# A two-layer graph network on one core: how the first batch's nodes and masks are brought in

## The chip, the cores and the metric

The kernel runs on one core of a Trainium2 chip. The core has five engines with queues of their own: TensorE (PE in the profile, with its weight loads as PEld), VectorE (DVE), ScalarE (ACT), GpSimd (POOL) and SyncE (SP). SP and ACT also issue transfers between DRAM and the core's memory, which 16 DMA engines carry out. The metric is the device time of one execution in microseconds; lower is better.

## The reference, cut to what matters

The input is x, 8 batches of 2048 nodes with 256 features, and adj, one 2048 x 2048 matrix of zeros and ones (int32) shared by all batches. The first layer is attention with 4 heads of 64. Its keys are cut into 8 chunks of 256, and each chunk has a softmax of its own:

```
q, k, v = x @ WqT + bq, x @ WkT + bk, x @ WvT + bv
scores = clip(q . k / 8, -10, 10)
scores = where(mask == 0, -10, scores)         # mask: adj by chunks
attn = softmax(scores, over the 256 of a chunk)
ctx = sum over chunks of attn @ v
x1 = layernorm(x + layernorm(ctx @ WoT + bo + x) * gamma + beta)
```

The second layer is a graph attention: Wh = x1 @ W, an edge score from the two nodes' own factors (sums of Wh times a_src and a_dst), a softmax over the neighbours where adj is not zero, an elu, a residual and a last layernorm.

## The kernel before, in words

The 16 tiles of 128 nodes are handled in 4 groups of 512. For every batch there is a projection per group (`project`): x is brought in with the features on the partitions (xT), and three matrix products make kT, the values (vaug) and qT. Then a loop of 64 slots runs over (query group q, pair of heads hp, key chunk c). In a slot, `scores` multiplies kT and qT into PSUM (ps), VectorE clips and masks with a slab of int8 limits (pr, line 382), ScalarE takes the exponential, and `product` multiplies with vaug (pc, line 406), which ScalarE copies out as raw; `normalize` divides (rd on VectorE, then a multiplication and an addition on GpSimd). Beside the slots, `Between` does the output projection and the two layernorms of the query group that went before. From batch 1 on the slots also carry the second layer of the batch before, line 722 and its tiles e; in batch 0 they don't.

In batch 0 the slots carry the masks instead. Both layers need adj turned, in two forms in DRAM: clipD, int8 limits of plus or minus 80 for the first layer, by query group, and edgeD, zeros and ones for the second. The class `Masks` makes them in 48 pieces (t, m): a piece is tile row t of adj and one of three banks m of 6, 5 and 5 column tiles. One call of `step` sends the stores of the piece before (SP), loads a new piece (SP, araw), turns an older piece on TensorE (pm, line 236), evicts it twice (clip on VectorE, line 238; edge on ScalarE, line 240), and compares a third piece with zero into bf16 (ab, line 226, on VectorE). A piece is loaded two steps before it is compared, and compared one step before it is turned. The pieces go row by row: t outermost, m inside.

The order of instructions on every engine is written out by hand: each engine runs them as the program issues them, and no scheduler moves them. The part ahead of the slots, the prologue, is at the end of the function: it calls load, turn, and the three products of each group in turn, with a mask step after nearly every piece, 17 steps in all, and then `finish_constants`. That function folds a_src and a_dst into eight more columns of the second layer's weights (lines 167 and 168, VectorE), and the value bias into bo and beta (four matmuls, line 178, and lines 185 and 189 on VectorE). After it come the loads of the first three slabs, and `scores(0)`.

x is loaded in the prologue as in later batches by `load_turned` (line 269): eight transfers of 64 KB per group, in runs of 32 floats, which put every square of 32 x 32 in its turned place. One VectorE transpose of such squares (`turned`, line 281) then completes xT. The kernel has a second way, `transposed` (lines 284 to 294), which it uses once in each batch for x1: the nodes lie plainly on the partitions, TensorE turns eight squares of 128 x 128 into PSUM, and ScalarE copies them out (line 293). `load_x` (line 260) is the plain load, one transfer of 512 KB, used for the residual.

Of the kernel before, what the change touches and what calls it, by code (L numbers as in the profile page):

```python
# [13 lines left out]
AF = mybir.ActivationFunctionType  # L14
ALU = mybir.AluOpType
# [7 lines left out]
def adj_resnorm_kernel(  # L23
# [19 lines left out]
    nc = tc.nc  # L43
    B, N, F = x.shape
    H, D = a_src.shape
    NT = N // P
    NCH = N // CH
# [8 lines left out]
    QT = CH // P  # L56
    CLIP = 10.0 * 8.0
    FAR = 100.0
    BANKS = (6, 5, 5)
# [103 lines left out]
    def finish_constants():  # L163
        for k, a_sb in enumerate(aa):
            for c in range(KC):
                wa = small.tile([P, F], F32, tag="ee", name="wa")
                nc.vector.tensor_mul(wa, w1_sb[:, c, :F], a_sb)
                nc.vector.tensor_reduce(
                    w1_sb[:, c, F + k * H : F + (k + 1) * H],
                    wa.rearrange("p (h d) -> p h d", h=H),  # L170
                    AX.X,
                    ALU.add,
                )


        pb0 = psM.tile([P, CH], F32, tag="psM", name="pb0")
        for c in range(KC):
            nc.tensor.matmul(
                pb0[:, :F],
                lhsT=bv_sb[:, c : c + 1].to_broadcast([P, P]),  # L180
                rhs=wo_sb[:, c, :],
                start=(c == 0),
                stop=(c == KC - 1),
            )
        nc.vector.scalar_tensor_tensor(
            bo_sb, pb0[:, :F], float(NK), bo_sb, op0=ALU.mult, op1=ALU.add
        )

        nc.vector.tensor_sub(beta_sb, beta_sb, bo_sb)
# [4 lines left out]
    def send():  # L194
        while outgoing:
            outgoing.pop(0)()


    class Masks:
# [1 line left out]


        def __init__(self):
            self.pieces = [(t, m) for t in range(NT) for m in range(len(BANKS))]
            self.raw, self.bits, self.done = [], [], []
            self.next = 0

        def step(self):
            send()
            if self.next < len(self.pieces):  # L210
                t, m = self.pieces[self.next]
                n, j0 = BANKS[m], FIRST[m]
                araw = ep.tile([P, WIDE * P], I32, tag="e", name="araw")
                nc.sync.dma_start(
                    out=araw[:, : n * P], in_=adj[t * P : (t + 1) * P, j0 * P : (j0 + n) * P]
                )
                self.raw.append((t, m, araw))
                self.next += 1
            if self.bits:
                t, m, ab = self.bits.pop(0)  # L220
                self.turn(t, m, ab)
            if len(self.raw) > 2 or (self.raw and self.next == len(self.pieces)):
                t, m, araw = self.raw.pop(0)
                w = BANKS[m] * P
                ab = small.tile([P, WIDE * P], BF16, tag="hh", name="ab")
                nc.vector.tensor_scalar(ab[:, :w], araw[:, :w], 0, None, ALU.not_equal)
                self.bits.append((t, m, ab))

        def left(self):
# [2 lines left out]
        def turn(self, t, m, ab):  # L232
            n, j0 = BANKS[m], FIRST[m]
            pm = psL.tile([P, WIDE, P], BF16, tag="psL", name="pm")
            for k in range(n):
                nc.tensor.transpose(pm[:, k, :], ab[:, k * P : (k + 1) * P], identb)
            clip = small.tile([P, WIDE, P], I8, tag="ee", name="clip")
            nc.vector.tensor_scalar(clip[:, :n], pm[:, :n], 2 * CLIP, -CLIP, ALU.mult, ALU.add)
            edge = small.tile([P, WIDE, P], U8, tag="hp", name="edge")
            nc.scalar.copy(edge[:, :n], pm[:, :n])  # L240
            q, u = t // QT, t % QT
            mi = max(k for k in range(len(BANKS)) if FIRST[k] <= t)
            at = (t - FIRST[mi]) * P

            def stores():
                nc.sync.dma_start(
                    out=clipD[q][:, j0 : j0 + n, u * P : (u + 1) * P], in_=clip[:, :n]
                )
                nc.sync.dma_start(out=edgeD[mi][:, j0 : j0 + n, at : at + P], in_=edge[:, :n])

            outgoing.append(stores)


    def by_node(dram, b, g):

        return dram[b, g * CH : (g + 1) * CH, :].rearrange("(t p) f -> p t f", p=P)

    def load_x(b, g, name):
        t = blocks.tile([P, QT, F], F32, tag="xb", name=name)
        nc.sync.dma_start(out=t, in_=by_node(x, b, g))  # L260
        return t

    def load_squares(dst, src):


        for c in range(src.shape[1] // P):
            for a in range(P // SQ):
                f0 = c * P + a * SQ
                nc.sync.dma_start(
                    out=dst[a * SQ : (a + 1) * SQ, c, :].rearrange("r (k s) -> r k s", s=SQ),  # L270
                    in_=src[:, f0 : f0 + SQ].rearrange("(k r) s -> r k s", r=SQ),
                )

    def load_turned(dram, b, g, name):
        t = blocks.tile([P, KC, CH], F32, tag="xb", name=name)
        load_squares(t, dram[b, g * CH : (g + 1) * CH, :])
        return t

    def turned(t, name):
        dst = blocks.tile([P, KC, CH], F32, tag="xT", name=name)  # L280
        nc.vector.transpose(dst.rearrange("p c n -> p (c n)"), t.rearrange("p c n -> p (c n)"))  # L281
        return dst

    def transposed(src, name):

        dst = blocks.tile([P, KC, CH], F32, tag="xT", name=name)
        pt = two_banks([P, KC, CH], "pt")
        for c in range(KC):
            for k in range(QT):
                nc.tensor.transpose(  # L290
                    pt[:, c, k * P : (k + 1) * P], src[:, k, c * P : (c + 1) * P], identf
                )
        nc.scalar.copy(dst, pt)  # L293
        return dst

    def project(b, g):

        cols = slice(g * CH, (g + 1) * CH)
        st = {}

        def load():
            st["x"] = load_turned(x, b, g, "xp")

        def turn():
            st["xT"] = turned(st["x"], "xT")

        def linear(dst, w, bias, apart=False):
            if apart:
                pps = [psL.tile([P, CH], F32, tag="psL", name="pp") for _ in range(KC)]
            else:  # L310
                pp = two_banks([P, KC, CH], "pp")
                pps = [pp[:, c, :] for c in range(KC)]
            for c in range(KC):
                for kc in range(KC):
                    nc.tensor.matmul(  # L315
                        pps[c],
                        lhsT=w[:, kc, c * P : (c + 1) * P],
                        rhs=st["xT"][:, kc, :],
                        start=(kc == 0),
                        stop=(kc == KC - 1),  # L320
                    )
            for c in range(KC):
                nc.scalar.activation(
                    dst[:, c, cols], pps[c], AF.Identity, bias=bias[:, c : c + 1]
                )

        def values():
            pv = two_banks([P, QT, F], "pv")
            for u in range(QT):
                for kc in range(KC):  # L330
                    nc.tensor.matmul(  # L331
                        pv[:, u, :],
                        lhsT=st["xT"][:, kc, u * P : (u + 1) * P],
                        rhs=wv_sb[:, kc, :],
                        start=(kc == 0),
                        stop=(kc == KC - 1),
                    )
            nc.scalar.copy(
                vaug[:, QT * g : QT * (g + 1), :, :D],
                pv.rearrange("p t (h d) -> p t h d", h=H),  # L340
            )

        return [
            load,
            turn,
            lambda: linear(kT, wk_sb, bk_sb),
            values,
            lambda: linear(qT, wq_sb, bq_sb, b > 0 and g == NCH - 1),
        ]
# [459 lines left out]
    masks = Masks()  # L809
    groups = [project(0, g) for g in range(NCH)]  # L810
    groups[0][0]()
    for _ in range(2):
        masks.step()
    groups[1][0]()
    for g in range(NCH):
        for k, piece in enumerate(groups[g][1:]):
            if k == 1 and 0 < g < NCH - 1:
                groups[g + 1][0]()
            piece()
            if g or k:  # L820
                masks.step()
    finish_constants()

# [41 lines left out]
    for b in range(B):  # L867
# [15 lines left out]
        for s in range(SLOTS):  # L883
            q, hp, c = where[s]
# [157 lines left out]
```

## Time and profile before

| what | value |
| --- | --- |
| median of 3 runs | 3862.64 us (3862.37 to 3863.09) |
| the profiled execution | 3862.74 us, of which its span 3861.0 us |
| busy share of the span | PE 96%, DVE 83%, ACT 51%, POOL 36% |
| TensorE's granted clock, mean | 0.991 |
| first matmul | 17.74 us after the span's start |
| first slot's first pr | 80.23 us |
| scores of the third slot | 88.65 us |
| slots with a mask step, first query group | 4.5 to 4.6 us each |
| mask comparison (line 226) | 48 times, 0.48 us for 640 columns, 0.55 for 768 |
| clip (line 238) and edge (line 240) | 0.82 and 0.68 us for 640 columns |
| normalization on GpSimd (lines 428, 430) | 1.05 and 1.28 us in a slot |

The span is the time from the first to the last instruction, and the execution is a little longer than it. Times within the profile count from the span's start. In a timeline a line gives the start, the duration, the engine and line, the operation with what it writes and reads, the number of instructions merged, and in brackets the idle time before it with what ended that. ACTq and SPq are the sequencers that issue transfers; the duration there is that of the issue, not of the transfer. Matmuls are pipelined and their ends modelled, so the start of the next instruction says more than the duration.

### The profile page before, as it was taken

To read this page: it belongs to the slowest core of one execution; us is meant where nothing else is said; L and a number is where in the kernel's file an instruction comes from. 1 tells how busy PE (TensorE), PEld (TensorE's weight loads), DVE (VectorE), ACT (ScalarE), POOL (GpSimd) and SP (SyncE) were. 2 spreads that over 40 slices of the span, in tenths; PEclk is the share of its full clock that TensorE was granted. 3 is DMA by queue.
4 is the path that set the end of the run, shared out by engine and by line. 5 is a ranking of instruction groups with operands and counts; after the bars stand their busy time and mean duration, and the time that the engine had idled before them with its cause. 6 is when DMAs were issued, how large, how long until landed. Compare 5 with 4: busy or idle time off the path is not lost. (4 is left out here: it accounts for less than half of the span.)

```text
span 3861.0 us, 160222 instructions
## 1 busy us (share of the span) xinstructions
PE 3687.8 (96%) x72068; PEld 2746.0 (71%) x72068; DVE 3204.6 (83%) x4810; ACT 1953.6 (51%) x3601; POOL 1387.4 (36%) x1202
## 2 busy tenths in 40 slices
PE   7999999999999999999999999999999999999787
PEld 4656677776777777776777767777677777776676
DVE  3877499986999779995999959998699977998798
ACT  3666445554555555554555545555455555555321
POOL 0445233332433333433433324343243333344310
PEclk9999999999999999999999999999999999999999
DMA  7642333333433333333433334333343433333344
GB/s 148 154 109 62 83 101 96 97 89 98 112 101 100 80 121 102 102 94 73 140 96 100 99 87 135 96 98 87 103 111 99 103 80 118 102 102 86 92 147 123
DMA packets 771328, 398.48 MB, mean 103 GB/s; under 512 B 442576, under 2 KB 735824, under 8 KB 770640
## 3 DMA queue, kind: packets, MB, share of 16 engines
q1 hardware_dynamic: 720640, 354.54, 36.3%
q10 hardware_dynamic: 50000, 33.70, 2.7%
q8 instruction: 563, 9.22, 1.0%
q14 instruction: 125, 1.02, 0.1%
HBM read 331.22 MB, written 56.89 MB: 101 GB/s over the span
## 5 line engine op out<-in xcount | busy, mean ns | idle before, releaser
L382 DVE SCALAR_TENSOR_TENSOR pr<-ps,slab 128x1024 f32<-128x1024 f32 x1024 | 1192.1, 1205 | 208.8 <-PE ps L371 206.7
L702 DVE SCALAR_TENSOR_TENSOR e<-srow,gd,et 128x640 f32<-128x640 f32 (+1 forms) x1536 | 1349.6, 934 | 17.9 <-DMA et<-edgeD 12.5
L406 PEld LDWEIGHTS pc<-vaug,pr 128*64 128x64 f32 x32768 | 1040.6, 138 | 445.5 <-issue 245.3
L406 PE MATMUL pc<-vaug,pr 128*64 128x65 f32 x32768 | 1157.9, 224 | 42.6 <-ACT raw L413 35.1
L394 ACT ACTIVATE pr<-pr 128x1024 f32<-128x1024 f32 x1024 | 1053.0, 1058 | 184.5 <-DVE pr L382 168.4
L722 PE MATMUL pa<-waug,e 128*64 128x65 f32 x32768 | 1081.5, 224 | 42.4 <-DVE e L702 40.0
L722 PEld LDWEIGHTS pa<-waug,e 128*64 128x64 f32 x32768 | 1020.1, 139 | 68.1 <-DVE e L702 39.8
L371 PE MATMUL ps<-qT,kT 64*128 64x512 f32 x4096 | 1027.4, 619 | 6.8 <-DVE pr L382 6.5
L428 POOL TENSOR_TENSOR part<-raw,rd 128x512 f32<-128x512 f32 x448 | 469.5, 1048 | 1462.1 <-DVE rd L421 1449.7
L413 ACT COPY raw<-pc 128x260 f32<-128x260 f32 x1024 | 384.9, 376 | 1157.7 <-PE pc L406 1132.2
L430 POOL TENSOR_TENSOR acc<-acc,part 128x512 f32<-128x512 f32 x448 | 574.9, 1283 | 35.1
L371 PEld LDWEIGHTS ps<-qT,kT 64*128 64x128 f32 x4096 | 351.3, 186 | 330.4 <-issue 209.7
L421 DVE RECIPROCAL rd<-raw 128x8 f32<-128x8 f32 x512 | 101.1, 197 | 116.7 <-ACT raw L413 113.0
L428 POOL TENSOR_TENSOR acc<-raw,rd 128x512 f32<-128x512 f32 x64 | 66.9, 1045 | 352.8 <-DVE rd L421 352.0
L750 ACT ACTIVATE hh<-pa,dn 128x64 f32<-128x64 f32 x512 | 114.4, 320 | 100.7 <-DVE dn L746 96.9
L315 PE MATMUL pp<-xT,wk_sb 128*128 128x512 f32 x256 | 124.1, 630 | 36.9 <-DVE xT L281 36.9
L565 PE MATMUL pw<-w_sb,x1T 128*128 128x264 f32 x512 | 138.7, 406 | 17.0 <-ACT x1T L293 9.0
L481 POOL TENSOR_TENSOR rs_c<-rs_c,nhalf 128x4 f32<-128x4 f32 x32 | 55.6, 1738 | 226.9 <-DVE off_c L480 226.9
L521 PE MATMUL po<-wo_sb,qT 128*128 128x256 f32 x512 | 125.5, 389 | 2.1 <-DVE qT L448 1.5
L315 PEld LDWEIGHTS pp<-xT,wk_sb 128*128 128x128 f32 x256 | 49.8, 200 | 94.3 <-issue 73.1
L315 PE MATMUL pp<-xT,wq_sb 128*128 128x512 f32 x256 | 116.0, 596 | 0.0
L331 PE MATMUL pv<-wv_sb,xT 128*128 128x256 f32 x512 | 115.9, 379 | 0.0
(90 smaller groups left out, 1885.1 us busy)
## 6 DMA issues: line engine op xcount, KB each, us to landing
et<-edgeD SPq DMA_DIRECT2D x256, 320.0 KB, 3.2
slab<-clipD SPq DMA_DIRECT2D x512, 128.0 KB, 3.6
et<-edgeD SPq DMA_DIRECT2D x128, 384.0 KB, 3.5
srow<-rowD SPq DMA_DIRECT2D x64, 320.0 KB, 4.4
xp<-in_x_dram SPq DMA_DIRECT2D x256, 64.0 KB, 2.3
xg<-in_x_dram SPq DMA_DIRECT2D x32, 512.0 KB, 4.7
x1D<-y ACTq DMA_DIRECT2D x32, 512.0 KB, 3.1
x1g<-x1D SPq DMA_DIRECT2D x32, 512.0 KB, 5.7
```

What stands on the lines that cost most here:

```text
L315: nc.tensor.matmul(pps[c], lhsT=w[:, kc, c * P : (c + 1) * P], rhs=st["xT"][:, kc, :], start=(kc == 0), stop=(kc == KC - 1),)
L371: nc.tensor.matmul(ps[:, k, :], lhsT=kT[rows, hp, t * P : (t + 1) * P], rhs=qT[rows, hp, cols], start=True, stop=True,)
L382: nc.vector.scalar_tensor_tensor(pr, pss[u], -CLIP, slab[:, u, :].unsqueeze(1).to_broadcast([P, 2, CH]), op0=ALU.max, op1=ALU.min,)
L394: nc.scalar.activation(pr, pr, AF.Exp, scale=0.125)
L406: nc.tensor.matmul(pc[z * D : (z + 1) * D, i, :], lhsT=probs[s][u][:, k, i * P + z * D : i * P + (z + 1) * D], rhs=vaug[:, KT * c + u, 2 * ...
L413: nc.scalar.copy(raws[s][:, k], pc)
L428: nc.gpsimd.tensor_mul(part, raw[:, :, :, :D], rd.to_broadcast([P, 2, QT, D]))
L430: nc.gpsimd.tensor_add(accv, accv, part)
L521: nc.tensor.matmul(po[:, k, :], lhsT=qT[:, c, t * P : (t + 1) * P], rhs=wo_sb[:, c, :], start=(c == 0), stop=(c == KC - 1),)
L565: nc.tensor.matmul(pw[:, k, : F + 2 * H], lhsT=self.x1T[:, c, u * P : (u + 1) * P], rhs=w1_sb[:, c, :], start=(c == 0), stop=(c == KC - 1),)
L702: nc.vector.scalar_tensor_tensor(e[:, :w], self.rows[n][:, :w], self.gd[:, h, j : j + 1], self.edge[k // JG][:, j % JG, :w], op0=ALU.max, ...
L722: nc.tensor.matmul(self.pa[z * D : (z + 1) * D, i * D1 : (i + 1) * D1], lhsT=e[:, i * P + z * D : i * P + (z + 1) * D], rhs=self.waug[:, j ...
```

## The change

It touches batch 0 alone. First, x is loaded plainly and turned by TensorE with `transposed` in the four projections of batch 0; other batches keep `load_turned`. The first two groups' loads are issued ahead of the first mask pieces. Second, the comparison of masks moves from VectorE to GpSimd and is turned around (equal to zero instead of not equal), so the clip's constants change sign, and the edge eviction becomes an activation that computes 1 - value. Third, the pieces go bank by bank within a query group: four tile rows of bank 0, then of bank 1, then of bank 2, then the next group. Fourth, no mask step follows the turning of a group, which leaves 14 steps in the prologue, and `finish_constants` is called between groups 2 and 3.

```diff
         def __init__(self):
-            self.pieces = [(t, m) for t in range(NT) for m in range(len(BANKS))]
+            self.pieces = [
+                (t, m) for q in range(NCH) for m in range(len(BANKS)) for t in range(QT * q, QT * (q + 1))
+            ]
...
-                nc.vector.tensor_scalar(ab[:, :w], araw[:, :w], 0, None, ALU.not_equal)
+                nc.gpsimd.tensor_scalar(ab[:, :w], araw[:, :w], 0, None, ALU.is_equal)
...
-            nc.vector.tensor_scalar(clip[:, :n], pm[:, :n], 2 * CLIP, -CLIP, ALU.mult, ALU.add)
+            nc.vector.tensor_scalar(clip[:, :n], pm[:, :n], -2 * CLIP, CLIP, ALU.mult, ALU.add)
...
-            nc.scalar.copy(edge[:, :n], pm[:, :n])
+            nc.scalar.activation(edge[:, :n], pm[:, :n], AF.Copy, bias=1.0, scale=-1.0)
...
         def load():
-            st["x"] = load_turned(x, b, g, "xp")
+            st["x"] = load_turned(x, b, g, "xp") if b else load_x(b, g, "xp")
 
         def turn():
-            st["xT"] = turned(st["x"], "xT")
+            st["xT"] = turned(st["x"], "xT") if b else transposed(st["x"], "xT")
...
     groups[0][0]()
+    groups[1][0]()
     for _ in range(2):
         masks.step()
-    groups[1][0]()
     for g in range(NCH):
         for k, piece in enumerate(groups[g][1:]):
             if k == 1 and 0 < g < NCH - 1:
                 groups[g + 1][0]()
             piece()
-            if g or k:
+            if k:
                 masks.step()
-    finish_constants()
+        if g == 2:
+            finish_constants()
```

## The prediction

> **What bounds the kernel now.** I read, in this order, the page, busy time by stretch, the ordered timeline of the first 90 us, the waits of those 90 us, and two slots of the first batch's loop. By the page TensorE is busy 96% of the span in 40 slices of which only the first and the last three fall clearly short of full.
>
> ```profile
> PE 3687.8 (96%) x72068; PEld 2746.0 (71%) x72068; DVE 3204.6 (83%) x4810; ACT 1953.6 (51%) x3601; POOL 1387.4 (36%) x1202
> ...
> PE   7999999999999999999999999999999999999787
> ```
>
> So time lost or won on TensorE before batch 1 should move the end one for one; the change touches nothing later. Busy time by stretch (columns: stretch, its length, PE, PEld, DVE, ACT, POOL busy, granted clock, DMA share, GB/s):
>
> ```profile
> 0.00:20.00 20.00, 2.26 (x3) 1.17 (x4) 1.80 (x2) 1.28 (x1) 1.34 (x10) 1.00 0.83 175
> ...
> 60.00:80.00 20.00, 14.88 (x65) 8.51 (x65) 10.76 (x21) 7.51 (x11) 0.00 (x0) 1.00 0.78 172
> 80.00:100.00 20.00, 18.49 (x254) 11.46 (x256) 14.00 (x19) 11.63 (x17) 3.45 (x4) 0.83 0.35 74
> 100.00:150.00 50.00, 50.00 (x877) 33.62 (x871) 40.47 (x56) 36.87 (x55) 24.25 (x21) 1.00 0.69 156
> ```
>
> TensorE is idle for nearly 18 us at the start and about 5 us around 77 to 82 us, then full. The timeline says what ends those gaps:
>
> ```profile
> 8.38 1.07 ACTq L160 DMA_DIRECT2D a_sb<-in_a_dst_dram  x1
> 9.48 1.28 ACT L323 ACT_TABLE_LOAD   x1 [9.48 <-DMA gamma_sb<-in_gamma_dram]
> ...
> 16.44 1.25 DVE L281 STREAM_TRANSPOSE xT<-xp 128x1024 f32<-128x1024 f32 x1 [16.44 <-DMA xp<-in_x_dram]
> ...
> 17.74 6.00 PE L315 MATMUL pp<-xT,wk_sb 128*128 128x512 f32 x8 [17.74 <-DVE xT L281]
> ```
>
> The eight 64 KB pieces of x (4096 packets of 128 bytes) land last; ScalarE has been free since 10.8. And where the loop starts:
>
> ```profile
> 72.81 1.38 SPq L358 DMA_DIRECT2D slab<-clipD  x3
> ...
> 79.89 0.43 DVE L189 TENSOR_TENSOR beta_sb<-beta_sb,bo_sb 128x256 f32<-128x256 f32 x1
> 80.23 2.35 DVE L382 SCALAR_TENSOR_TENSOR pr<-ps,slab 128x1024 f32<-128x1024 f32 x2
> ...
> 81.51 3.79 PE L371 MATMUL ps<-qT,kT 64*128 64x512 f32 x8 [4.98 <-DVE pr L382]
> ```
>
> The first softmax tile waits behind finish_constants on VectorE (74.86 to 80.2), and the scores after it take 3.79 us where later ones take 1.99. The waits of these 90 us add the third loss, at each change of group:
>
> ```profile
> PE pm L236 <- DVE ab L226: 4.2, 3, 1.5
> ```
>
> **What the Trainium skill says.** "GPSIMD Engine Reference", Engine selection, calls one-input elementwise work there roughly line rate, and its Performance pitfalls give 1.0 to 2.0 cycles per element for compare bodies; at the page's 1.2 GHz that is, as an estimate, 0.5 to 1.3 us for 640 or 768 elements. The trace has no such operation. "ScalarE: Activation LUTs", What ACT_TABLE_LOAD costs: 1283 ns, plus about 1380 ns of drain; the trace agrees with the first (1.28), and shows nothing queued close behind the load, so not the second. "TensorE: Matmul & The Clock Gate", Why this matters for your kernels: keep idle gaps under about 3 us; here a 4.98 us gap was followed by halved speed, a 3.21 us gap at 317 us was not (the scores right after took 1.99).
>
> **The change, part by part**, on the profiled execution's own time, 3862.74 us (span 3861.0 and 1.74 around it; median of the runs shown 3862.64, so 0.1 lower).
>
> *Start.* One plain 512 KB load replaces eight small-packet loads: SP's 13.4 us of issuing become about 1, and VectorE's 1.25 us transpose becomes eight TensorE transposes (1.09 us) and one ScalarE copy (1.01 us, 1.06 from its start to the next matmul; both rows exist at 436 to 438 us). x no longer comes last, but the copy is ScalarE work, and ScalarE first issues its 13 loads and loads its table. In the changed program's order, DMA completions rotate through eight semaphores: bv's issue waits for the first x, gamma's for the second, w1's for the first mask piece, a_dst's for the second mask piece. By then four SP loads (1.84 MB) and four weights (1.05 MB) have moved, 2.9 MB. The trace moved 204 GB/s on average from 2.6 to 12 us, with slices up to 345. Counted from 2.6 us that ends at 11 to 17; I take 13.3, since large packets fill the engines better. Then a_dst 0.8, table 1.28, copy 1.06: first matmul at 16.4 instead of 17.74, **−1.3** (ends: 14.3, −3.4; 21.5 at the slow rate and with the drain, +3.8). The loads of groups 1 to 3 take SP 5.5, 4.4 and 5.0 us now and about 0.5 each after; behind them stand mask loads and stores, for which TensorE does not wait, so that is worth nothing. Uncovered it would be worth their difference, 13 us.
>
> *Three changes of group.* Before, from the last query matmul to the next key matmul: 2.91, 2.98 and 3.11 us, of which two mask pieces (0.45 each), the comparison and the transpose. After: one mask piece (0.45 to 0.5), then transposes to +1.6; ScalarE does its two query evictions (to about +1.35), the edge eviction (0.58 to 0.7) and the copy (1.06), which gives +3.05 to +3.15. At the third, finish_constants' four matmuls (1.08) come first: +3.9. Sum **+1.1** (ends 0 and +3). The comparison, 48 × 0.48 or 0.55 = 24 us of VectorE, is on GpSimd, idle here from 2 us on.
>
> *finish_constants.* Its 5.5 us of VectorE, one wait for a mask store included, go between two clips some 7 us apart, where VectorE has nothing else; without that gap they would hold the next clip, and cost at most 5.5. The first pr then waits for its slab: issued 0.44 us before the last query matmul ends (73.25), landed about 3.9 later, 3.6 after that end where it is now 7.0. **−3.4** (ends −5, −1.5). TensorE's gap shrinks to about 2.3 us, so its clock should hold: warm, the third scores follow the first pr by 6.3 us, now 8.4 (80.23 to 88.65): **−2.1** (ends −2.1, 0).
>
> *Mask pieces.* 14 instead of 17 steps in the prologue, so 37 instead of 34 in the loop. What a step costs there is seen from two slots:
>
> ```profile
> 97.65 1.99 PE L371 MATMUL ps<-qT,kT 64*128 64x512 f32 x8
> ...
> 102.11 1.99 PE L371 MATMUL ps<-qT,kT 64*128 64x512 f32 x8
> ```
>
> 4.46 us with a piece, against 3.94 between scores at 304.52 and 308.46 without: 3 × 0.52 = **+1.6** (the pieces' matmuls in the prologue are already taken out above). Bank by bank, a slab needs at most pieces stored one slot (4.5 us) before its own issue; stores land in 2.2 us, so this order costs nothing; if one were late, a slot would lose about 2 us once. The inverted clip and edge constants change no shape.
>
> *Loop with the comparison moved.* GpSimd works 1.05 + 1.28 of each 4.55 us slot. For the comparison I take 1.1 us (between the skill's ends; the two-input rows here, 2.0 to 2.5 ns per element, bound it at 1.3 to 1.9). 3.4 fits in 4.55. Behind it queue the next normalization, on whose reading of raw ScalarE waits two slots later. VectorE gains 0.5 us a slot, yet TensorE is full there: of its waits for the mask slots (3.5 us for edge, 1.0 for pr) I give **−0.4** (ends −3, +3).
>
> Sum: −1.3 + 1.1 − 3.4 − 2.1 + 1.6 − 0.4 = −4.5; 3862.74 − 4.5 = 3858.2, against the median 3858.1.
>
> **Rivals.** (1) *GpSimd becomes the bound.* If a comparison takes more than 4.55 − 2.33 = 2.2 us, each of some 36 slots stretches by the excess. At 2.35 us the gain is gone, at 2.55 the kernel is slower by over 0.2%, at 3.0 it takes 3858 + 36 × 0.8 = 3887. For it: GpSimd here needs 1.0 to 2.0 us for a power of four elements a partition, so some operations are slow there. Against: its masked select of 128 elements takes 0.29 us, 1.5 ns per element after a memset's 0.1 us floor. (2) *The start really is freed.* If loads overlap so well that x's transposes and ScalarE's table set the time, the first matmul comes at 9.48 + 1.28 + 1.06 + 0.1 = 11.9: 4.5 more, 3853.6. Against it stands the order of semaphores. (3) *The loop start stays cold or the slabs late* (first pr at +5.5, clock halved): 4 us of gain go, 3862.
>
> **How the numbers follow.** Likeliest 0.70: 3858.1, own range 3853.8 to 3862. Rival 1: 0.12, rival 2: 0.09, rival 3: 0.09. About 0.2%, 7.7 us, is what a measurement of this kernel can tell from no change: faster means under 3854.9, slower over 3870.4. Rival 2 and a tenth of the likeliest lie below: 0.16. Rival 1 above its 2.55 us and a little for the unforeseen: 0.12. The rest, 0.72, is the same. The range 3852.5 to 3865 leaves out rival 1's upper part and the tails.
>
> **What would show it.** Right: the first L315-type matmul at 15 to 18 us, released by ScalarE's copy, with the table load just before that; first pr at 3.4 to 4 us after the last query matmul, released by its slab's DMA; the next scores at 2 us, granted clock near 1.0 from 80 to 100; slots with masks still 4.5 us; GpSimd's comparison near 1.1 us. Wrong: a comparison over 2.2 us with ACT raw waiting for POOL, or the first matmul before 13 or after 20 us, or VectorE's pr slowed beside GpSimd.

## The result

The changed kernel takes 3857.56 us (median of four runs, 3856.91 to 3860.71), the kernel before, run beside it, 3862.86; the ratio is 0.9988, 95% interval 0.997 to 1.0005. Four runs leave the sign open. Run again, 18 times against 38, it takes 3856.91 us against 3862.29: **ratio 0.9986, interval 0.9979 to 0.9993**. The change makes the kernel faster by 0.14%, some 5.4 us. The forecast was 3858.1, a gain of 4.5.

The profiled execution is the slowest of the first four, 3860.71 us with a span of 3858.9; the profile of the second set has a span of 3854.7. Executions of one kernel differ by several microseconds (3854.69 to 3861.87 in the second set), so what follows counts differences at the same point of the prologue and not between ends.

The page of the changed kernel (busy time of each engine, share of the span, instructions):

```profile
PE 3696.8 (96%) x72100; PEld 2759.2 (72%) x72100; DVE 3178.8 (82%) x4758; ACT 1955.9 (51%) x3605; POOL 1475.8 (38%) x1250
```

TensorE has 32 more matmuls (the transposes), VectorE 52 fewer instructions (48 comparisons and four transposes), GpSimd 48 more. Busy time by stretch of the changed kernel (columns: stretch, its length, PE, PEld, DVE, ACT, POOL busy, granted clock, DMA share, GB/s):

```profile
0.00:20.00 20.00, 6.17 (x14) 3.46 (x15) 0.00 (x0) 2.29 (x2) 5.59 (x12) 1.00 0.74 230
20.00:40.00 20.00, 18.09 (x75) 11.32 (x74) 2.87 (x3) 8.14 (x11) 6.06 (x3) 0.91 0.38 84
...
80.00:100.00 20.00, 20.00 (x371) 13.95 (x369) 13.89 (x17) 14.14 (x22) 13.83 (x10) 1.00 0.56 120
```

The last row is what the forecast promised: 80 to 100 is full at a granted clock of 1.00, where it was 18.49 us busy at 0.83. The second is not: the clock is 0.91 from 20 to 40, where it was 1.00 in the kernel before:

```profile
20.00:40.00 20.00, 17.98 (x71) 10.65 (x70) 6.27 (x9) 7.69 (x11) 0.00 (x0) 1.00 0.71 129
```

The timeline of the changed kernel (start, duration, engine and line, operation, number merged, idle before it and what ended that; lines in between are left out here and below) shows the three places. The start:

```profile
5.85 1.94 PE L292 MATMUL pt<-identf,xp 128*128 128x128 f32 x8 [5.85 <-DMA xp<-in_x_dram]
12.27 1.12 ACTq L160 DMA_DIRECT2D a_sb<-in_a_dst_dram  x1
13.41 1.28 ACT L295 ACT_TABLE_LOAD   x1 [13.41 <-DMA gamma_sb<-in_gamma_dram]
14.71 1.01 ACT L295 COPY xT<-pt 128x1024 f32<-128x1024 f32 x1
15.77 5.36 PE L318 MATMUL pp<-xT,wk_sb 128*128 128x512 f32 x8 [7.99 <-ACT xT L295]
```

x has landed and is turned by 7.8 us; then TensorE waits 7.99 us for a copy that ScalarE can't begin, because its queue is still issuing constants. Those issues wait until earlier transfers have landed: bo's, at 9.57, for the value weights (landed at 9.55), and a_dst's, at 12.27, for the second mask piece (landed at 12.24). A change of group:

```profile
28.25 0.50 PE L238 MATMUL pm<-identb,ab 128*128 128x128 bf16 x6
...
30.48 1.01 ACT L295 COPY xT<-pt 128x1024 f32<-128x1024 f32 x1
31.54 5.40 PE L318 MATMUL pp<-xT,wk_sb 128*128 128x512 f32 x8 [1.91 <-ACT xT L295]
```

Between the two stand the transposes (28.58) and the copy. The same eight matmuls take 3.70 us in the last group; here they ran at reduced speed. And the start of the loop:

```profile
73.02 0.44 PE L238 MATMUL pm<-identb,ab 128*128 128x128 bf16 x5
...
76.05 4.81 DVE L385 SCALAR_TENSOR_TENSOR pr<-ps,slab 128x1024 f32<-128x1024 f32 x4 [1.73 <-DMA slab<-clipD]
77.33 2.26 PE L374 MATMUL ps<-qT,kT 64*128 64x512 f32 x8 [1.66 <-DVE pr L385]
```

The first pr is released by its slab and not by VectorE's other work, and the scores after it run at nearly full speed (2.26 us where it was 3.79). Put together, at the third scores (88.65 before, 82.07 now) the kernel is ahead by 6.58 us:

| part, from where to where | before, us | after, us | difference |
| --- | --- | --- | --- |
| span's start to first key matmul | 17.74 | 15.77 | -1.97 |
| first key matmul to last query matmul's end | 55.51 | 57.25 | +1.74 |
| that end to the first pr | 6.98 | 3.03 | -3.95 |
| first pr to the third scores | 8.42 | 6.02 | -2.40 |

The second row holds the changes of group (3.29, 3.05 and 3.33 us, before 2.91, 2.98 and 3.11: +0.67), the slow product (+1.70) and a first key product of 5.36 instead of 6.00 us (-0.64), which sum to +1.73.

The column of before is one execution, and it is a late one. In the two other kernels here that start as the kernel before does (the constants moved alone, the order of the pieces alone) the first key matmul comes at 16.68 and 17.03 us; in the six that start as the changed one it comes at 15.75 to 16.33. By these means the start is worth 1.1 us and not 1.97. The kernel with the order alone, which has the old start and the old loop's start, reaches its third scores at 87.45 us; against it the changed kernel is ahead by 5.4 us and not by 6.58.

In the loop the comparison on GpSimd takes 1.6 to 1.9 times the 1.1 us that was forecast. GpSimd's groups by shape (count, busy us and mean ns of one, idle before):

```profile
L228 POOL TENSOR_SCALAR ab<-araw 128x640 bf16<-128x640 int32 x32 | 57.9, 1808 | 26.3 <-PE pm L238 20.2 <-issue 6.0
L228 POOL TENSOR_SCALAR ab<-araw 128x768 bf16<-128x768 int32 x16 | 34.1, 2129 | 22.5 <-PE pm L238 12.6 <-DMA araw<-in_adj_dram 8.2 <-issue 1.7
```

It is hidden all the same, at first almost without slack. Stretches of the loop in the changed kernel (columns as above):

```profile
85.00:160.00 75.00, 74.80 (x1289) 50.25 (x1285) 54.32 (x68) 55.59 (x83) 66.93 (x48) 1.00 0.71 161
160.00:260.00 100.00, 91.03 (x1387) 60.26 (x1384) 71.13 (x101) 63.34 (x105) 73.08 (x55) 0.97 0.64 144
```

In the first 75 us GpSimd works 66.93 and TensorE 74.80: next to nothing is lost. In the next stretch the layernorms join GpSimd's queue, and TensorE waits:

```profile
188.60 2.01 POOL L484 TENSOR_TENSOR rs_a<-rs_a,nhalf 128x4 f32<-128x4 f32 x1 [0.86 <-DVE off_a L483]
...
190.86 1.82 POOL L228 TENSOR_SCALAR ab<-araw 128x640 bf16<-128x640 int32 x1
192.74 0.45 PE L238 MATMUL pm<-identb,ab 128*128 128x128 bf16 x5 [2.58 <-POOL ab L228]
```

The power operation (2.01 us for four elements a partition) stands ahead of the comparison, itself waiting 0.86 us for VectorE, and the mask pieces wait for all of it. Waits of TensorE for the masks between 85 and 260 us in the changed kernel (total us, times, longest):

```profile
PE pm L238 <- POOL ab L228: 5.1, 3, 2.6
PE pm L238 <- ACT edge L242: 1.7, 2, 1.4
```

Together 6.8 us; in the same stretch of the kernel before it was 3.5, all for the edge eviction:

```profile
PE pm L236 <- ACT edge L240: 3.5, 4, 1.6
```

Over the first 56 slots (from GpSimd's first normalization to that of the eighth round of eight slots) the kernel before takes 281.71 us, the changed one 284.24 in this profile and 282.15 in the second: the loop gives back 0.4 to 2.5 us of the 6.58. The 2.1 us between these two profiles lie in slots 40 to 47 (39.83 and 37.77 us), where the first has the granted clock halved for 3.4 us, at 316 us, and the second has not. The kernel with the order alone takes 280.02 us. So what the loop costs is known to some 2 us at best.

### The profile page after: what moved, and what is told of

It is laid out like the page before. It is cut to its first block, busy times and chain, and to the rows that moved or that the text cites. A ratio compares the mean times of both kernels' runs of the same rounds, so it can differ in the third digit from the quotient of the medians.

```text
span 3858.9 us, 160304 instructions
## 1 busy us (share of the span) xinstructions
PE 3696.8 (96%) x72100; PEld 2759.2 (72%) x72100; DVE 3178.8 (82%) x4758; ACT 1955.9 (51%) x3605; POOL 1475.8 (38%) x1250
## 5 line engine op out<-in xcount | busy, mean ns | idle before, releaser
L568 PEld LDWEIGHTS pw<-w_sb,x1T 128*128 128x128 f32 x512 | 90.2, 190 | 35.0 <-ACT x1T L295 10.9
```

Source lines behind the costliest of these rows:

```text
L568: nc.tensor.matmul(pw[:, k, : F + 2 * H], lhsT=self.x1T[:, c, u * P : (u + 1) * P], rhs=w1_sb[:, c, :], start=(c == 0), stop=(c == KC - 1),)
```

## The experiments

The theory: the gain is made at the start and at the loop's start, the mask edits are neutral, and the start is still held by ScalarE's issuing of constants. The rivals: the gain comes from the load alone or the constants alone; the comparison on GpSimd helps (VectorE relieved) or costs.

**The changed kernel again**, unedited, as the reference for all that follows.

> The changed kernel once more, nothing edited: it says how far one profiled execution and one median can be trusted. Both theories: 3857.5 us, within 1.5. In its profile the first matmul of the key product at 15.8 us and the third slot's scores at 82 us. If the second group's key product, which took 5.40 us in the one profile (3.70 in the groups after it), takes 3.7 here, that was the clock of one execution; if 5.4 again, it belongs to the change and costs 1.7 us.

Measured: 3856.91 us, ratio 0.9986 [0.9979, 0.9993]; first key matmul at 16.02, third scores at 82.35, so 6.30 ahead at that point. The second group's key product is slow again (31.88, 5.40 us).

**The comparison back on VectorE.**

```diff
-                nc.gpsimd.tensor_scalar(ab[:, :w], araw[:, :w], 0, None, ALU.is_equal)
+                nc.vector.tensor_scalar(ab[:, :w], araw[:, :w], 0, None, ALU.is_equal)
```

> The changed kernel with the comparison back on VectorE, its sense and all else kept. Theory: the comparison of 1.8 to 2.1 us makes mask turns wait for GpSimd where a power stands ahead of it (2.58 and 2.38 us in two slots of the second query group); without these, and with some of the old waits for the edge eviction back (about 2 us), 3854.5 to 3856. Rival, as the prediction had it: on GpSimd it is hidden, and VectorE's relief is worth 0.4 us: 3858 here, no wait for GpSimd to win back.

Measured: 3857.52 us, 0.9987 [0.998, 0.9994]: no difference from the changed kernel. The waits between 85 and 260 us of this kernel:

```profile
PE pm L238 <- ACT edge L242: 4.3, 5, 1.6
```

GpSimd no longer appears among them, but the edge evictions hold the mask pieces for longer instead (4.3 against 1.7). The gain that I had expected of it did not come; where the comparison runs makes no difference that these runs can tell.

**The comparison twice.** GpSimd issues each comparison two times over, into the same tile; the second is only extra work.

```diff
                 nc.gpsimd.tensor_scalar(ab[:, :w], araw[:, :w], 0, None, ALU.is_equal)
+                nc.gpsimd.tensor_scalar(ab[:, :w], araw[:, :w], 0, None, ALU.is_equal)
```

> The changed kernel with every GpSimd comparison done twice, so 3.6 to 4.3 us of it in a slot beside 2.33 of normalization. Theory (rival 1 of the prediction, tried on purpose): GpSimd bounds the slots with masks: about 6.1 us a slot instead of 4.53 and some 36 slots, so 50 to 60 us slower than the changed kernel, 3908 to 3918. If GpSimd's time were really hidden, or the slots had more slack than its sum says, under 3880.

Measured: 3894.71 us, 1.0084 [1.007, 1.0098], 31.7 us more than the kernel before beside it, so some 37 more than the changed kernel, and less than I had expected. The first of those stretches in this kernel:

```profile
85.00:160.00 75.00, 59.87 (x992) 38.98 (x986) 44.32 (x54) 42.44 (x65) 73.15 (x49) 0.98 0.54 123
```

and a slot of it in the timeline (left out at the mark is the normalization's addition, 1.28 us):

```profile
109.20 1.04 POOL L432 TENSOR_TENSOR part<-raw,rd 128x512 f32<-128x512 f32 x1
...
111.56 1.81 POOL L228 TENSOR_SCALAR ab<-araw 128x640 bf16<-128x640 int32 x1
113.45 1.81 POOL L229 TENSOR_SCALAR ab<-araw 128x640 bf16<-128x640 int32 x1
115.23 1.05 POOL L432 TENSOR_TENSOR part<-raw,rd 128x512 f32<-128x512 f32 x1
115.32 0.45 PE L239 MATMUL pm<-identb,ab 128*128 128x128 bf16 x5 [1.49 <-POOL ab L229]
```

Now GpSimd is the bound: 73.15 of 75 us, its operations end to end, one slot every 6.03 us, and TensorE drops to 59.87. So the mechanism of the prediction's first rival exists, and at one comparison the kernel stands just below it: 1.05 + 1.28 + 1.81 = 4.14 us in slots of 4.5, or 4.46 with 768 columns. Its price was set too high. The eight slots from the first normalization on take 48.8 us here against 36.5 in the changed kernel, +12.3, and the next eight 49.4 against 36.8, +12.6; but slots 16 to 23 take 51.8 against 45.7, +6.1, and slots 24 to 31 50.3 against 44.6, +5.7. From slot 16 on the projections and layernorms of finished query groups already stretch a slot to 5.6 or 5.7 us, and half of the extra work fits in there.

**The late constants.** The loads that the first groups don't need (woT, bv, bo, gamma, beta, w1, a_src, a_dst) leave ScalarE's queue for SP's, after group 0.

```diff
-        nc.scalar.dma_start(out=a_sb, in_=a.rearrange("h d -> (h d)").partition_broadcast(P))
...
+    def late_loads():
+        nc.sync.dma_start(out=wo_sb, in_=woT.rearrange("(c p) f -> p c f", p=P))
+        ...
+            nc.sync.dma_start(out=a_sb, in_=a.rearrange("h d -> (h d)").partition_broadcast(P))
...
+        if g == 0:
+            late_loads()
         if g == 2:
             finish_constants()
```

> The changed kernel with the eight loads that ScalarE issues last (wo, bv, bo, gamma, beta, w1, a_src, a_dst) moved to SP's queue after the first group. Theory: in the changed kernel ScalarE's issues, waiting for semaphores of SP's big loads, held the table load and the copy; now the table load comes at about 4 us, the copy right after the transposes (7.8), the first matmul at about 9 instead of 15.8, and the kernel at 3851. Rival: the transfers' volume sets the start, with the key weights landing late: first matmul at 13 or later, 3855 or more.

Measured: 3851.08 us, 0.9967 [0.9956, 0.9979], from six runs between 3846.12 and 3854.9. The timeline of this kernel:

```profile
3.80 1.28 ACT L300 ACT_TABLE_LOAD   x1 [3.80 <-issue]
...
7.63 1.01 ACT L300 COPY xT<-pt 128x1024 f32<-128x1024 f32 x1 [2.55 <-PE pt L297]
8.70 5.94 PE L323 MATMUL pp<-xT,wk_sb 128*128 128x512 f32 x8 [1.10 <-ACT xT L300]
```

ScalarE's table is loaded at 3.8 us, its copy follows the transposes at once, and the first key product begins at 8.70: 7.1 us earlier. What held the start was the queue of issues on ScalarE, and not x: its transposes start at 5.66 us here and at 5.85 in the changed kernel. At the third scores (77.64) 4.4 of the 7.1 are left in this profile: 0.8 goes in the groups, of which the third now has the slow product (39.53, 5.40 us); 0.7 at the first pr, which its slab releases 3.69 us after the last query matmul and not 3.03; and 1.2 because the scores after it are slow (3.44 us).

**Both: late constants and the comparison on VectorE**, the two diffs above together, run in two sets.

> Both edits together: late loads and the comparison on VectorE. Theory: the gains are at different places and add up: 3848 to 3849.5. Rival: what the start wins is given back at the loop's beginning, since the first slabs or mask pieces then come late: 3853 or more.

> Late loads and the comparison on VectorE once more, unedited, beside others on the same chip. Theory: 11 to 12 us faster than the kernel before, as in the first call. Rival: that ratio was one chip's, and it is under 9 here.

Measured: 3850.55 us, 0.9972 [0.9961, 0.9984], and 3853.79, 0.9976 [0.9965, 0.9986]; third scores at 74.03 and 73.72, 8 us before the changed kernel's. The gains do not quite add up: 3848 to 3849.5 was expected of the first set, and 11 to 12 us less than the kernel before of the second, where it is 9.4. This kernel, the one with the late constants alone and the last one below are the fastest here, a quarter to a third of a per cent faster than the kernel before; between them the intervals do not choose.

**The constants moved, alone**, in the kernel before:

```diff
+        if g == 2:
+            finish_constants()
-    finish_constants()
```

> The kernel before, with the call of finish_constants alone moved between groups 2 and 3. Theory: the parts hang together. Here the last group is still turned on VectorE, behind those ten operations and their wait for a mask store; what the loop's start wins (first pr 3 to 4 us after the last query product instead of 7, and a warm clock, 5 to 6 us in all), the last group's key product loses by waiting 4 to 6 us: 3861 to 3863. Rival, the prediction's sum read part by part: the 5.5 us are its own, 3857.

Measured: 3864.93 us, 1.0007 [0.9999, 1.0015]: no gain. The timeline of this kernel:

```profile
57.43 0.50 PE L236 MATMUL pm<-identb,ab 128*128 128x128 bf16 x6
...
63.28 0.43 DVE L189 TENSOR_TENSOR beta_sb<-beta_sb,bo_sb 128x256 f32<-128x256 f32 x1
63.63 1.24 DVE L281 STREAM_TRANSPOSE xT<-xp 128x1024 f32<-128x1024 f32 x1
64.92 5.28 PE L315 MATMUL pp<-xT,wk_sb 128*128 128x512 f32 x8 [5.09 <-DVE xT L281]
```

Where x is turned on VectorE, the ten operations of the constants (59.26 to 63.7) stand ahead of the last group's transpose: this change of group takes 7.49 us instead of 3.11, and the product after it runs slowly. The wait has only moved, from the loop's start to the last group.

**The plain load and turn, alone**, in the kernel before:

```diff
-            st["x"] = load_turned(x, b, g, "xp")
+            st["x"] = load_turned(x, b, g, "xp") if b else load_x(b, g, "xp")
...
-            st["xT"] = turned(st["x"], "xT")
+            st["xT"] = turned(st["x"], "xT") if b else transposed(st["x"], "xT")
```

> The kernel before, with the plain load and the turn on TensorE and ScalarE alone. Theory: the first matmul comes at about 16, 1.7 us earlier, the changes of group cost about what they did, and the loop's start is as before (first pr 7 us after the last query product): 3860.5 to 3862. Rival: the load is the part that wins: 3858 or less.

Measured: 3863.74 us, 1.0002 [0.9994, 1.001]: no difference, where I had expected a small gain. The first key matmul comes at 15.76, as in the changed kernel, so the earlier issue of the second group's load, which is left out here, adds nothing at that point. But its product takes 6.56 us, and the first pr stays at 80.01 behind the constants (80.23 before). What is won at the start is gone by there: among the constants' operations VectorE waits for a mask store, until 78.42 us here and 78.65 before, so coming earlier only makes that wait longer (1.87 us, before 1.08).

**The changed kernel with the constants at the end of the prologue**, as in the kernel before:

```diff
-        if g == 2:
-            finish_constants()
+    finish_constants()
```

> The changed kernel with the call of finish_constants put back to the end of the prologue. Theory: the loop's start is the change's main term; the first pr waits for those operations again and comes 7 us after the last query product instead of 3, TensorE's clock is slow after it, the third slot's scores come 5.5 us later, less the 1.0 us that the four matmuls cost between groups: kernel 3861 to 3863. Rival: the slabs' landing was the bound all along and the start of the loop moves by under 2 us: 3859 or less.

Measured: 3862.31 us, 0.9998 [0.999, 1.0006]. The timeline of this kernel at the loop's start:

```profile
73.04 0.44 PE L238 MATMUL pm<-identb,ab 128*128 128x128 bf16 x5
...
78.65 2.35 DVE L385 SCALAR_TENSOR_TENSOR pr<-ps,slab 128x1024 f32<-128x1024 f32 x2
79.93 3.21 PE L374 MATMUL ps<-qT,kT 64*128 64x512 f32 x8 [3.61 <-DVE pr L385]
...
86.12 1.99 PE L374 MATMUL ps<-qT,kT 64*128 64x512 f32 x8
```

The prologue ends where it did (73.04 against 73.02), the first pr comes 2.6 us later, the scores after it are slow, the third scores come 4.05 us later, and the kernel loses nearly all of its gain. So the loop's start carries the gain. With the turn still on VectorE, where the constants moved alone, these runs did not have it.

**The order of the pieces alone** (in the kernel before), **and the mask step after the turn put back** (17 steps, in the changed kernel).

```diff
-            self.pieces = [(t, m) for t in range(NT) for m in range(len(BANKS))]
+            self.pieces = [
+                (t, m) for q in range(NCH) for m in range(len(BANKS)) for t in range(QT * q, QT * (q + 1))
+            ]
```

> The kernel before with the pieces bank by bank and nothing else. Theory: no slab waited for a piece before and none does after, so no difference: 3863 within 1.5. Rival: four wide pieces in a row, or stores closer to the slabs that read them, cost or gain a wait in the slots: over 3 us either way.

```diff
-            if k:
+            if g or k:
                 masks.step()
```

> The changed kernel with the mask step after a group's turn put back, so 17 steps in the prologue. Theory: its matmuls fill the wait for ScalarE's copy but need a comparison that GpSimd ends only then, so each change of group costs 0.5 us more and three steps of 0.52 us leave the loop: no difference, 3857 within 1. Rival: they are free there, and the kernel gains 1.6 us, 3855.5.

Measured: 3861.72 us, 0.9995 [0.9987, 1.0003], and 3858.37 us, 0.9987 [0.9981, 0.9994]: neither tells from its base.

**All that looked good together**: late constants, the comparison on VectorE, and 17 steps.

> Late loads, the comparison on VectorE, and the mask step after a group's turn put back (17 steps in the prologue). Theory: that step's matmuls run while TensorE waits for ScalarE's copy of the turned nodes, so they are free, and three steps leave the loop: 3 x 0.52 = 1.6 us less than the 3850.6 of the run without it, 3849. Rival: the step's evictions delay the copy or the next evictions at every change of group, and nothing is won: 3850.5 or more.

Measured: 3853.14 us, 0.9976 [0.9968, 0.9984], no better than without the three steps in the loop, where 1.6 us had been expected. In its profile the first pr comes at 70.14 (68.00 without them), and the scores after it are slow, 3.58 us.

## Why the prediction was right

The time, 3858.1 for 3857.56 and 3856.91, held, and so did most of the working. How near it came is in part luck: a slow product of 1.7 us was not foreseen, and four terms that each came out 0.3 to 0.7 us better than counted, with a first product that happened to be shorter, more than covered it. Term by term:

- *Start, -1.3.* Measured -1.97, and -1.7 in the second profile; by the means of all kernels with either start -1.1. The order of issues was as described: the last one, a_dst's, began at 12.27 where 13.3 was counted and took 1.12 instead of 0.8; the table took 1.28, the copy to the matmul 1.06. The drain counted in the slow end did not show: the copy starts 0.02 us after the table load. The late constants, with 8.70, show that nothing else held the start until then. Rival 2, a start freed by itself, did not happen, for the reason given against it.
- *Changes of group, +1.1.* Measured +0.67; the third took 3.33 where 3.9 was counted. But the step priced the waits and not the matmuls after them: at the second group they took 5.40 instead of 3.70 us, +1.7, and that was not foreseen. The first product, 0.64 us quicker than before, covered part of it; that one is not the change's, since it takes 5.24 to 6.11 us in the kernels with the changed start and 5.50 to 6.76 in those with the old one.
- *finish_constants, -3.4.* Measured -3.95 (3.03 us to the first pr, released by the slab, where 3.6 was counted). The gap between two clips held all of it, as the step said; the constants alone in the kernel before show what it costs where the gap isn't free, 4.4 us at the last group and a slow product.
- *The clock kept, -2.1.* Measured -2.40; against the order alone, where the clock was halved for 3.4 us and not for 6.8 as before, -1.4.
- *Mask pieces +1.6 and loop -0.4.* Together +1.2; measured between +0.4 and +2.5, and +2.1 to +4.2 against the order alone, so the profiles don't settle it. Here the step that failed is "for the comparison I take 1.1 us": it is 1.81 and 2.13, above the 0.5 to 1.3 us that I had worked out from the Trainium skill, "GPSIMD Engine Reference", Engine selection and Performance pitfalls, and above what the trace's two-input rows were said to bound it at (1.6 us for 640 elements, 1.9 for 768). The nearest rows of the trace itself, the two-input operations at 2.0 to 2.5 ns per element, were closer to the 2.8 ns per element that it takes. The mis-sizing cost nothing that these runs can tell, because what was left of the slot was enough: with the comparison back on VectorE the time was the same.
- *Rival 1* was nearer than its 12% said: 2.13 us against a limit of 2.2. Doubling the comparison reaches it, at some 37 us. By the rival's own formula it would be (3.62 - 2.2) x 36 = 51 us with the narrow pieces' time for all; the step "each of some 36 slots" failed, since the slots from the 16th on are longer and leave GpSimd room.
- *Rival 3* (the loop's start slow, 4 us lost) is what the constants at the end gave, at 4.05 us, and it was not the changed kernel.

The sum to the third scores was -5.7, measured -6.58 and -6.30; the end was -4.5, measured -5.4.

Which product runs slowly is not set by the code alone, and the kept traces show what it hangs on. In every one of them the granted clock is recorded as 1.00 or 0.50, and it changes only at instants that lie whole multiples of 3.41 us apart: in the changed kernel at 19.15, 32.80, 36.22 and 193.23 us, after 4, 1 and 46 such stretches. (Before its first change the view shows 1.00, though the first product runs at half pace until then.) Where the boundaries lie against the program differs from execution to execution. These are stretches of the changed kernel:

```profile
29.39:32.80 3.41, 1.50 (x6) 0.68 (x4) 0.35 (x1) 2.04 (x3) 1.63 (x1) 1.00 1.11 291
32.80:36.22 3.42, 3.42 (x5) 1.35 (x4) 0.00 (x0) 0.00 (x0) 0.00 (x0) 0.50 0.34 74
```

And these of the kernel with the comparison on VectorE:

```profile
27.46:30.87 3.41, 2.89 (x18) 1.62 (x16) 1.36 (x2) 1.67 (x4) 0.00 (x0) 1.00 0.79 158
30.87:34.28 3.41, 2.01 (x5) 1.06 (x6) 0.06 (x1) 1.34 (x2) 0.00 (x0) 1.00 1.08 258
34.28:37.70 3.42, 3.42 (x17) 2.20 (x16) 1.36 (x2) 1.58 (x3) 0.00 (x0) 1.00 0.21 50
```

Both kernels leave TensorE idle for 1.91 us before the second group's key product. In the first this gap falls into one stretch, which leaves 1.50 us of work in it, and the next stretch gets half the clock. In the second the boundary at 30.87 divides the gap, and the clock stays. Eight profiles have this gap of 1.91 us. In four (the changed kernel twice, the constants at the end, the comparison twice) it lies in one stretch, and the next one is halved; in the other four (the comparison on VectorE, the late constants, and both together in two sets) a boundary divides it, and no halving follows. Counted over the first 90 us of all 14 profiles, the 14 stretches at full clock that a halved one followed had at most 1.56 us of TensorE's work, and the 255 others at least 1.60. In the loop further on the two overlap (1.40 us kept the clock, 1.71 lost it). So the 1.7 us are no fixed cost of the change but depend on the execution. The gap at the loop's start, 1.66 us, leaves at least 1.75 us of work in any stretch that is otherwise full; by these figures, as an estimate, the clock is kept there wherever the boundaries lie.

"TensorE: Matmul & The Clock Gate", What's actually happening, in the Trainium skill says that the clock follows activity in windows of some 3.4 us that run freely, whatever the kernel does; the traces agree, with their 3.41 us. Its PE-mode transpose says that transposes don't count as activity in the same way. That does not fit here: if the transposes are left out of the count, a stretch with 0.34 us of other matmuls kept the clock (the last kernel above, 37.13 us), and one with 1.56 us lost it (the constants alone, 81.78 us).

## What to carry to other kernels

A wait that is removed from an engine's queue is worth something only if the next work on that queue isn't the next thing waited for: the constants moved alone won nothing, with the turn moved to other engines they carried the gain. When a load lands early and its consumer still waits, look at what else the consumer's engine has to issue first; here 7 us lay in transfers that nobody needed yet. For an operation that the trace doesn't show, price it by the nearest measured row of the same engine, and compare it with the room in the tightest slot. Before a slow product is charged to a change, look whether a second execution has it too, and where the boundaries of the clock's stretches lie in each.

## What had not been expected of the hardware

- A one-input comparison on GpSimd, int32 to bf16, costs 1.81 us for 128 x 640 and 2.13 us for 128 x 768; VectorE does them in 0.48 and 0.55 us.
- The speed of TensorE after a short idle gap can't be read from the gap alone: scores took 2.26 us after 1.66 us idle (changed kernel) and after 2.02 us (comparison on VectorE), 3.44 after 2.31 (late constants), 2.82 after 3.34 (constants moved alone), 3.21 after 3.61 (constants at the end). What decides is how much of the gap falls into one stretch of 3.41 us, and how much of the scores into the halved stretch after it.
- ScalarE's first operation began 0.02 us after its table load ended.
